# Returned rows of the first experts: an accumulating transfer of GpSimd in place of a load and VectorE's add

## The chip, the core and the metric

The kernel runs on one core of one Trainium2 chip. Its engines are TensorE (PE, with its weight loads PEld), VectorE (DVE), ScalarE (ACT), GpSimd (POOL) and SyncE (SP), which here only issues transfers. The metric is the time of the program on the device in microseconds (us), as the median of repeated runs.

## What is computed

The kernel is a decoder of two layers on `x` of 8 batches, 256 tokens and 256 features, all in float32. Each of six blocks normalizes the rows and adds its result to `x`:

```
x = x + L0_attn(layernorm(x))             # 16 heads
x = x + L0_xattn(ctx, layernorm(x))       # 16 heads, no weights
x = x + L0_ffn(layernorm(x))              # the first experts
x = x + L1_attn(layernorm(x))             # causal
x = x + L1_xattn(layernorm(x), ctx)
x = x + L1_ffn(layernorm(x))              # the second experts
```

The change is in the third block:

```
g = sinkhorn(x @ gate_w, 8 iterations)          # 256 tokens x 8 experts
vals, idx = top_k(g over tokens, 32)            # each expert chooses 32 tokens
out = (x[idx] @ experts[e]) * vals
back = zeros.at[idx].set(out)                   # a token chosen by several experts keeps the last one
```

so that `x + back` is the input of the second layer.

## The kernel before

The residual rows stay in SBUF for the whole run, in the tile `x` of 128 partitions by 16 row tiles by 256 features; batch b owns the row tiles 2b and 2b+1. The first two layers' attentions are 24 units: for each pair of batches two self attentions and two cross attentions of the first layer, then eight causal self attentions of the second layer. Their score products (`st`, L330), exponentials (`pT`, L341) and value products (`o`, L367) give the beat, four steps to a unit. Between the steps stand jobs, in an order written out by hand in `order_of_jobs`: `st16` takes the statistics of unit 16 (L249), `no16` normalizes (`xn`, L258, on POOL), `ro16` transposes (`tr`, L287), and so on. `x0` to `x3` advance the first experts of one pair of batches by one step each, up to the next `yield` of the generator `chosen_experts`. Every engine, and each queue of transfers, follows this order strictly.

For one pair of batches the generator normalizes the rows (`xnb`), writes them to DRAM (`xn<-xnb`, L657), and makes eight rounds of the gates: a product `cs` on PE, then `rc`, `gc`, `rsum` and `rr` on DVE (L676 to L682). DVE picks the 32 best of each expert (`top`, L698 to L703). SP writes these to DRAM and loads them in other layouts (`slots`, `idx_row`, `by_half`). For each batch, POOL gathers the chosen rows (`gather`, L735) in two indirect transfers, PE transposes them (`tr<-rows`) and multiplies by the experts (`y`, L751), DVE works out which rows must go aside because a later expert chose the same token (`junk`, L763), ACT or DVE scales (`ys`), and POOL scatters the result in two indirect transfers (L785) to `returned[b]` in DRAM. The second scatter waits for the first.

Then SP loads the first 256 rows of `returned[b]` (L795, 256 KB) into the tile `back`, which has two buffers, and DVE adds it to `x` (L798). The reader of the sum is the `st` job of the second layer's unit of the same batch (L249).

SP's queue carries more than that: the loads `memk` and `memv` of the cross attentions (L534, L536), and, one expert for every second unit, `packs` (L235 to L240), which copies the second experts' weights, 2.1 MB for each, from DRAM to DRAM in another layout. When the last expert step is done, `weights_x` closes the pools of the first experts and loads the weights of the second cross attention in their room: `wkv_x`, `wq_x` and `wout_x` on POOL's queue (L826 to L828), `nkrow`, `nvcol`, `lns` and `lnb` on SP's (L831 to L838). `own` (L863, L864) is a small DVE product with `nvcol`.

Of the kernel before, what the change touches and what calls it, by code (L numbers as in the profile page):

```python
# [29 lines left out]
F32 = mybir.dt.float32  # L30
# [4 lines left out]
ALU = mybir.AluOpType  # L35
# [4 lines left out]
P = 128  # L40
B, S, D = 8, 256, 256
# [116 lines left out]
def plain(  # L158
# [4 lines left out]
    nc = tc.nc  # L163
# [118 lines left out]
    def transposed(rows, work, mm, tag, dst=None, bufs=2):  # L282

        ps = mm.tile([P, 2, 2 * P], F32, tag="mm", name="tr")
        for t in range(2):
            for c in range(2):
                nc.tensor.transpose(ps[:, c, t * P : (t + 1) * P], rows[:, t, c * P : (c + 1) * P], ident)  # L287
        if dst is None:
            dst = work.tile([P, 2, 2 * P], F32, tag=tag, name=tag, bufs=bufs)
        nc.scalar.copy(dst, ps)  # L290
        return dst
# [310 lines left out]
    bwork = w_exp.enter_context(tc.tile_pool(name="b2", bufs=2, side="right"))  # L602
# [8 lines left out]
    returned = [dram.tile([2 * S, D], F32, name=f"back{b}") for b in range(B)]  # L611
# [32 lines left out]
    def chosen_experts(b0, nb):  # L644
# [86 lines left out]
        def gather(b):  # L731
            gathered[b] = bwork.tile([P, 2, D], F32, tag="rows", name="rows")
            for h in range(2):
                q = 2 * b + h
                nc.gpsimd.indirect_dma_start(  # L735
                    out=gathered[b][:, h, :],
                    out_offset=None,
                    in_=kept[b][:, :],
                    in_offset=bass.IndirectOffsetOnAxis(ap=from_i[:, q : q + 1], axis=0),
                )  # L740
# [3 lines left out]
        for b in range(nb):  # L744
            rT = transposed(gathered[b], bwork, mm, "rT")
            yield
            y = mm.tile([P, 2, D], F32, tag="mm", name="y")
            for e in range(E):
                rows = slice(TOP * (e % 4), TOP * (e % 4) + TOP)
                for c in range(2):  # L750
                    nc.tensor.matmul(  # L751
                        y[rows, e // 4, :],
                        rT[:, c, TOP * e : TOP * (e + 1)],
                        experts[:, e, c, :],
                        start=c == 0,
                        stop=c == 1,
                    )
                if e == 3:
                    yield
            for h in range(2):  # L760
                q = 2 * b + h
                junk = bwork.tile([P, S], F32, tag="junk", name="junk")
                nc.vector.scalar_tensor_tensor(  # L763
                    junk,
                    idx_row[:, b, :],
                    col[:, 0, q : q + 1],
                    later[:, h, :],
                    ALU.is_equal,
                    ALU.mult,
                    accum_out=over[:, q : q + 1],  # L770
                )
            of_b = slice(2 * b, 2 * b + 2)
            nc.vector.scalar_tensor_tensor(to[:, of_b], over[:, of_b], 0.0, to[:, of_b], ALU.is_equal, ALU.mult)
            nc.vector.tensor_tensor(to_i[:, of_b], to[:, of_b], aside, ALU.add)
            ys = bwork.tile([P, 2, D], F32, tag="ys", name="ys")
            for h in range(2):
                q = 2 * b + h
                if b0:
                    nc.scalar.activation(ys[:, h, :], y[:, h, :], AF.Copy, scale=col[:, 1, q : q + 1])
                else:  # L780
                    nc.vector.tensor_scalar(ys[:, h, :], y[:, h, :], col[:, 1, q : q + 1], None, ALU.mult)
            yield
            for h in range(2):
                q = 2 * b + h
                nc.gpsimd.indirect_dma_start(  # L785
                    out=returned[b0 + b][:, :],
                    out_offset=bass.IndirectOffsetOnAxis(ap=to_i[:, q : q + 1], axis=0),
                    in_=ys[:, h, :],
                    in_offset=None,
                )  # L790
                if not h and b + 1 < nb:
                    gather(b + 1)
                yield
            back = bwork.tile([P, 2, D], F32, tag="back", name="back")
            nc.sync.dma_start(back, returned[b0 + b][:S].rearrange("(t p) d -> p t d", p=P))  # L795
            yield
            xb = x[:, 2 * (b0 + b) : 2 * (b0 + b) + 2, :]
            nc.vector.tensor_tensor(xb, xb, back, ALU.add)  # L798
            yield


# [122 lines left out]
    for n, u in enumerate(units):  # L924
# [20 lines left out]
        "tb0": lambda: by_dims(sinT1, wides[2]),  # L945
    }
    ex = [chosen_experts(2 * i, 2) for i in range(B // 2)]
    jobs |= {f"x{i}": partial(next, ex[i], None) for i in range(B // 2)}
    order_of_jobs = """
# [2076 lines left out]
```

## Time and profile before

| | before |
|---|---|
| median of 16 runs | 1130.0 us (1124.93 to 1135.34) |
| the profiled execution | 1129.51 us |
| its span, first to last instruction | 1127.7 us |
| mean granted TensorE clock | 0.994 |
| scatters to `returned` (L785, 16) | 176.8 to 341.7 us, 1.0 us each on POOL |
| loads of `back` (L795, 8) | 184.0 to 344.2 us, 0.37 us each to issue |
| adds (L798, 8) | 188.1 to 352.1 us, 0.68 us each |

The profile is one execution. A page of it lists the busy time of each engine, the chain of work that ended last, followed back from the end, and the costliest groups of instructions. Other views are a timeline of each engine (start, length, engine, line, operation, output and inputs, and in brackets the idle time before it and what ended it), busy times in chosen windows, and a list of who waited for whom. PE's busy time is modelled, so a full PE is not a PE at its peak. Times are in us from the start of the span.

### The profile page before, as it was taken

What the parts mean: (1) busy time and instruction counts of PE and PEld (TensorE: products, weight loads), DVE (VectorE), ACT (ScalarE), POOL (GpSimd) and SP (SyncE); (2) the same over time, 40 slices, a digit from 0 to 9 for tenths busy, and PEclk for the clock granted to TensorE, in tenths of its full rate; (3) what the DMA queues carried; (4) which work ended last, traced back from release to release, by engine and by line L of the source; (5) the groups of instructions that cost most, each with busy time, mean ns of one, the idle gap of its engine ahead of it and who ended that gap; (6) DMA issues with size and microseconds to landing.
All of it is one profiled execution on the core that took longest, in us unless ns stands there. A gap on an engine that the chain in (4) does not pass through costs nothing.

```text
span 1127.7 us, 34931 instructions
## 1 busy us (share of the span) xinstructions
PE 1083.7 (96%) x15186; PEld 712.6 (63%) x15186; DVE 592.3 (53%) x1573; ACT 460.7 (41%) x747; POOL 439.5 (39%) x519
## 2 busy tenths in 40 slices
PE   6999999998998999999999999999999999999997
PEld 3444545544544545676777776777775768888874
DVE  5576778878887446435444443434357572222213
ACT  4776767674554524242424232323232321322220
POOL 3456364647687414242424233333325133000014
PEclk9999999999999999999999999999999999999999
DMA  8048344234145100101010102020232045999924
GB/s 238 32 158 283 108 135 126 63 121 135 35 140 203 73 3 20 40 21 49 21 50 20 49 21 49 20 49 20 49 122 52 1 170 195 360 415 402 393 65 139
DMA packets 62819, 130.87 MB, mean 116 GB/s; under 512 B 9904, under 2 KB 45984, under 8 KB 58304
## 3 DMA queue, kind: packets, MB, share of 16 engines
q1 hardware_dynamic: 54944, 108.61, 28.4%
q0 software_dynamic: 4992, 16.92, 4.3%
q10 hardware_dynamic: 2720, 3.02, 0.8%
q8 instruction: 121, 1.98, 0.7%
q14 instruction: 42, 0.34, 0.1%
HBM read 110.03 MB, written 35.80 MB: 129 GB/s over the span
## 4 chain that ended last, share of the span: by engine, by line
PE 80%; DVE 9%; ACT 4%; POOL 2%; DMA 2%; issue 2%; SPq 0%; DVEq 0%; ACTq 0%; POOLq 0%
PE h L272 8%; PE k L272 7%; PE st L330 7%; PE v L272 6%; PE o L367 4%; PE wo L272 4%; PE ox L1594 4%; PE stx L1554 4%; PE out L2014 4%; PE out L1831 4%; PE h L1196 3%; PE q L272 3%; PE qk L278 3%; ACT pT L341 3%; PE ao L278 2%
## 5 line engine op out<-in xcount | busy, mean ns | idle before, releaser
L341 ACT ACTIVATE pT<-st 128x1024 f32<-128x1024 f32 (+1 forms) x128 | 110.4, 915 | 59.8 <-PE st L330 58.3
L367 PE MATMUL o<-pT,padv 128*32 128x256 f32 (+1 forms) x1536 | 96.6, 368 | 1.4 <-DVE by_q L383 1.0
L1560 POOL TENSOR_TENSOR both<-pTx 128x512 f32<-128x512 f32 x64 | 87.4, 1395 | 21.1 <-ACT pTx L1558 19.1
L272 PE MATMUL h<-xrT,w 128*64 128x128 f32 (+1 forms) x1936 | 87.1, 250 | 0.7 <-issue 0.7
L272 PEld LDWEIGHTS h<-xrT,w 128*64 128x64 f32 x1936 | 84.5, 137 | 3.6 <-issue 1.3
L1189 DVE TENSOR_TENSOR midr<-sl,h 128x128 f32<-128x128 f32 x102 | 29.4, 288 | 101.8 <-PE h L272 69.2
L341 ACT ACTIVATE pT<-st,kbias 128x1024 f32<-128x1024 f32 x64 | 67.8, 1111 | 31.5 <-PE st L330 29.8
L367 PEld LDWEIGHTS o<-pT,padv 128*32 128x32 f32 x1536 | 44.4, 110 | 53.4 <-issue 22.6
L1558 ACT ACTIVATE pTx<-stx 128x1024 f32<-128x1024 f32 x64 | 62.5, 1023 | 31.4 <-PE stx L1554 28.1
L1188 ACT ACTIVATE sl<-h 128x128 f32<-128x128 f32 (+1 forms) x114 | 35.3, 310 | 95.0 <-PE h L272 56.0
L330 PE MATMUL st<-qm,kT 32*128 32x512 f32 (+1 forms) x512 | 67.3, 594 | 5.2 <-ACT qm L309 2.1
L278 PE MATMUL qk<-xnT,l_wqkv 128*32 128x256 f32 x1024 | 66.9, 387 | 0.8 <-issue 0.8
L1554 PE MATMUL stx<-qTx,kTx 64*128 64x256 f32 x512 | 64.4, 391 | 2.1 <-ACT pTx L1558 2.1
L1594 PE MATMUL ox<-pTx,vx 128*32 128x256 f32 x1024 | 63.2, 380 | 0.0
L1649 POOL TENSOR_TENSOR oT<-oT,rs 128x512 f32<-128x512 f32 x30 | 37.6, 1286 | 61.9 <-DMA rs<-rd 61.9
L383 DVE STREAM_TRANSPOSE by_q<-o 128x512 f32<-128x512 f32 x48 | 34.0, 709 | 51.2 <-PE o L367 51.0
L1554 PEld LDWEIGHTS stx<-qTx,kTx 64*128 64x128 f32 x512 | 46.1, 186 | 20.4 <-issue 7.0
L254 POOL TENSOR_TENSOR lxrs<-lxve,mhalf 128x2 f32<-128x2 f32 x8 | 5.6, 705 | 127.6 <-DVE lxve L252 127.6
L346 POOL TENSOR_SCALAR_AFFINE_SELECT pT<-pT 128x512 f32<-128x512 f32 x64 | 41.7, 671 | 29.9 <-ACT pT L341 29.5
L278 PEld LDWEIGHTS qk<-xnT,l_wqkv 128*32 128x32 f32 x1024 | 33.5, 112 | 28.6 <-issue 9.8
L2014 PE MATMUL out<-w,midr 128*64 128x256 f32 x408 | 47.6, 380 | 1.5 <-issue 1.3
L1602 DVE COPY oT<-ox 128x512 f32<-128x512 f32 x16 | 11.0, 689 | 72.3 <-PE ox L1594 72.3
(397 smaller groups left out, 2240.9 us busy)
## 6 DMA issues: line engine op xcount, KB each, us to landing
w<-packs SPq DMA_DIRECT2D x22, 1408.0 KB
w<-packs SPq DMA_DIRECT2D x22, 768.0 KB
rs<-rd SPq DMA_DIRECT2D x16, 512.0 KB
packs<-L_ffn_w_eDF SPq DMA_DIRECT2D x8, 704.0 KB
packs<-L_ffn_w_eDF SPq DMA_DIRECT2D x8, 640.0 KB
packs<-L_ffn_w_eFD SPq DMA_DIRECT2D x8, 640.0 KB
ctxT<-ctx_T SPq DMA_DIRECT2D x8, 512.0 KB
wkv_x<-L_xattn_Wkv POOLq DMA_DIRECT2D x1, 4096.0 KB
```

The source lines that it names most:

```text
L272: nc.tensor.matmul(out[h], lhsT[:, h], rhs, start=start, stop=stop, skip_group_check=True)
L278: nc.tensor.matmul(out[h : h + HP], lhsT[:, h : h + HP], rhs, start=start, stop=stop, skip_group_check=True)
L330: nc.tensor.matmul(st[:, r, :, :n], self.kT[rows, c, bass.ts(kt, P)], self.qm[rows, :, c, q0:], start=True, stop=True,)
L341: nc.scalar.activation(pT[:, :, :, :n], st[:, 2 * k : 2 * k + 2, :, :n], AF.Exp, scale=self.scale, **kb)
L346: nc.gpsimd.affine_select(out=pT[:, :, :, :P], in_=pT[:, :, :, :P], compare_op=ALU.is_ge, fill=0.0, base=0, pattern=[[0, 2], [0, 2], [1, P ...
L367: nc.tensor.matmul(o[HP * j : HP * j + HP, m, q0:], self.v_pad[:, kt, 8 * c + 2 * j + m, :], pTs[j // 2][:, j % 2, m, : S - q0], start=kt ...
L1554: nc.tensor.matmul(st[:, g, kt, :], kT[rows, c, bass.ts(kt, P)], qT[rows, c, :], start=True, stop=True)
L1558: nc.scalar.activation(pT, st, AF.Exp, scale=scale)
L1560: nc.gpsimd.tensor_tensor(both, pT[:, :, 0, :], pT[:, :, 1, :], ALU.add)
L1594: nc.tensor.matmul(o[at : at + HP, i, :], v[:, kt, 2 * (c2 + i) + g, lo : lo + HP], pT[:, g, kt, :], start=kt == 0, stop=kt == 1, skip_gro ...
L1831: nc.tensor.matmul(ps, mid[:, i, lo : lo + P], w2[:, i, :], start=i == 0, stop=i == NFC - 1)
L2014: nc.tensor.matmul(ps[h], mid[:, i, h], sets[k % len(sets)][1][:, i, :], start=i == 0, stop=i == NFC - 1, skip_group_check=True,)
```

## The change

The load of `back` on SP, the tile, and DVE's add are gone. At the place of the add, POOL issues one transfer from `returned[b]` to the rows of `x` that adds to its destination.

```diff
-            back = bwork.tile([P, 2, D], F32, tag="back", name="back")
-            nc.sync.dma_start(back, returned[b0 + b][:S].rearrange("(t p) d -> p t d", p=P))
             yield
             xb = x[:, 2 * (b0 + b) : 2 * (b0 + b) + 2, :]
-            nc.vector.tensor_tensor(xb, xb, back, ALU.add)
+            nc.gpsimd.dma_start(xb, returned[b0 + b][:S].rearrange("(t p) d -> p t d", p=P), accum_op=ALU.add)
             yield
```

The steps of the generator stay as many as they were, so the hand-written order is the same; the step that held the load is empty. In the order of instructions PE and ACT are as before; DVE has lost its eight adds, SP its eight loads, and POOL has eight more transfers. One instruction has moved: L864 now stands right behind L863 on DVE, where ten others stood between them. The transfer waits for the second scatter to land, and the first statistics of the batch wait for the transfer.

## The prediction

> **What bounds the kernel now.** I read the page first: the parts on busy time, the slices and the chain. TensorE holds the end, but the change lies between 176 and 358 us, so I then read that stretch by windows, by the chain in order of time, and by each engine's timeline.
>
> From the page:
>
> ```profile
> span 1127.7 us, 34931 instructions
> PE 1083.7 (96%) x15186; PEld 712.6 (63%) x15186; DVE 592.3 (53%) x1573; ACT 460.7 (41%) x747; POOL 439.5 (39%) x519
> PE 80%; DVE 9%; ACT 4%; POOL 2%; DMA 2%; issue 2%; SPq 0%; DVEq 0%; ACTq 0%; POOLq 0%
> ```
>
> Time is gained only where PE now stands idle in this stretch, and lost wherever PE is made to wait anew. The windows (columns: length, then PE, PEld, DVE, ACT, POOL busy, granted clock, DMA share, GB/s):
>
> ```profile
> 180.00:190.00 10.00, 10.00 (x228) 5.84 (x220) 7.18 (x23) 9.12 (x13) 3.91 (x5) 1.00 0.56 146
> 190.00:200.00 10.00, 9.64 (x187) 5.08 (x190) 9.04 (x33) 7.31 (x11) 6.58 (x8) 1.00 0.54 192
> 270.00:275.00 5.00, 2.33 (x24) 1.14 (x16) 4.93 (x11) 1.04 (x2) 4.81 (x6) 1.00 0.56 202
> 275.00:280.00 5.00, 5.00 (x60) 2.47 (x52) 0.86 (x5) 2.87 (x5) 3.04 (x4) 0.66 0.16 56
> ```
>
> At 190 us PE and DVE are both nearly full and feed each other. At 271 us there is the one real hole, and after it the granted clock falls to 0.66. The timelines of DVE, POOL and PE at the first add (batch 0):
>
> ```profile
> 188.09 0.67 DVE L798 TENSOR_TENSOR x<-x,back 128x512 f32<-128x512 f32 x1
> 188.80 0.43 DVE L249 BATCH_NORM_STATS2 lnst<-x 128x6 f32<-128x256 f32 x1
> 190.59 0.18 DVE L682 RECIPROCAL rr<-rsum 128x4 f32<-128x4 f32 x1
> 188.28 1.62 POOL L419 TENSOR_TENSOR qs<-qs,sinT 128x512 f32<-128x512 f32 x1 [4.94 <-DVE qs L416]
> 191.13 0.44 PE L278 MATMUL cs<-g,rr 128*32 128x8 f32 x32
> ```
>
> The statistics L249 read batch 0's rows at once after the add, and PE's `cs` product waits for `rr`, five DVE steps later. Last, from the chain, the two transfers that hold DVE and PE up today:
>
> ```profile
> 236.51 5.49 DMA back<-ys,to_i
> 242.02 2.85 DMA back<-back
> 267.29 6.73 DMA rows<-xn,from_i
> ```
>
> **What goes.** Eight adds on DVE (median 0.68 us, about 0.6 of it serial, since neighbours overlap), their 4.0 us of waits for the load, and eight loads on SP (0.37 us to issue). SP's gain is larger than that: its L795 waits for the scatter to land, 94.5 us in eight times, and the weight copies `packs`, `memk`, `memv` and `nkrow` stand behind it. They move forward.
>
> **What comes.** Eight issues on POOL at the places of the old adds. No row shows an accumulating transfer. Issue: the nearest row is the direct `xr` load, 0.55 us; upward, an indirect one at 1.0. Issue to landing: at the low end 2.4 to 2.6 (scatters of 128 KB in quiet), or 2.85 for the same 256 KB through SP; at the high end 6.5 to 7.1, which `rows` gathers take under a `packs` copy. A cost below nothing is excluded, since each add's reader now waits for a transfer where it waited for a 0.67 us instruction. I take 4.0: the 2.85 row plus about 1 us, because the transfer must also read its destination.
>
> The Trainium skill, DMA: Bandwidth & Descriptors, "Anatomy of one DMA — SWDGE (gpsimd) path", fits a plain GpSimd transfer as 2.0 us plus bytes over 436 GB/s; an estimate from it is 2.6 us for 256 KB, which would take 1.4 us off each wait below, and it prices no accumulation. Its "Rules for kernel authors" say to issue a transfer early and wait on it late, which speaks against this change.
>
> **Term 1, batch 0: +6.1.** POOL reaches the accumulating transfer when L419 ends, at 189.7 to 189.9; it lands at 193.7. DVE stands at L249 until then, with the whole router iteration queued behind it. From the start of L249 to the end of `rr` take 2.0 us (188.80 to 190.77), so `rr` comes at 195.7. PE is ready for `cs` at 191.1 and runs in order, so it is idle for 4.6 us. The clock follows: after the hole of 2.03 and 0.64 us at 271, 32 matmuls of `y` took 3.55 us, against 1.97 at full clock. I add 1.5. At a landing of 2.6 the hole is 3.2, at 7.0 it is 7.6.
>
> The Trainium skill, TensorE: Matmul & The Clock Gate, "What's actually happening", puts the threshold at an idle window of about 3.4 us; the row at 271 shows the fall after shorter holes, so I go by the row. By the page a hole of 3.2 might cost no clock, the forecast's 4.6 would.
>
> **Term 2, batch 2's gathers: +1.0 (0 to 3.5).** Without batch 1's load, which waits until 229.4, the next `packs` copy follows `memv` at 212.5 instead of 229.9. It takes 10 to 11 us (230 to 240 in the windows), so the gathers at 218.9 and 220.3 now run in its tail. Gathers at the same distance from a copy's start, 315.4 and 317.0 after 309.2, took 4.6 and 3.1; PE wants the rows at 223.2. So 0.3 to 2 us, or 3.5 if they take 6.6 as those at 232.5 did.
>
> **Term 3, batches 1, 2 and the hole at 271: -2.9 (0 to -5.6).** The scatters at 229.9 and 236.5 are then quiet. The second accumulating transfer goes at 233.7 and lands near 237.7, when its reader (238.35 less one add) comes. The third goes behind `lnrs`, at about 240.1, and lands at 244.1; the reader stood at 246.56, so DVE gains 2.5. PE has only 1.5 to 1.8 of idle to give back before 265. The gathers at 265.9 come 1.5 earlier, and the `packs` copy of 262.2 some 6 earlier, since batch 3's load no longer holds it; they land at 268.8 and the hole closes. That would be worth 5.6 at the end of `y`. But POOL is full there (4.81 of 5): second `xnb`, then 0.8 for the fourth issue, then the selects that the next `o` product needs. That brings `o` to 276.0 instead of 278.9.
>
> **Term 4, batch 4: +0.5 (-0.6 to +1.2).** Issue at 296.5, after `xn`; landing 300.5; the reader is due at 299.3 to 299.9. POOL's selects behind it slip by 0.1 to 0.3.
>
> **Term 5, batches 5 to 7: +2.3 (0 to +4).** Batch 5's transfer comes behind the scatter and its gap, at 331.5, and lands at 335.5; its reader was at 331.2. DVE is 4.3 late, POOL's `xn` ends at 340.4 instead of 336.1, and PE's transposes of it, due at 336.6, wait 3.8 and lose 1.5 of clock. Part comes back: DVE's `own` product now stands right behind its reduction (338.0), and its operand `nvcol` is loaded sooner, so the 2.57 us wait at 346.4 and PE's holes of 1.33 (350.5) and 1.62 (356.1) go. I followed DVE to `kT` L473 before 356: PE is 2.3 late there. Batch 6's landing is hidden by that delay, batch 7's (351.1 plus 4) by DVE's work until 358.1.
>
> Batch 3 costs nothing but the 0.8 in term 3: its reader comes at 291.6, 15 us after the issue. If that cover were gone it would cost a landing, 4.0.
>
> **Sum.** 6.1 + 1.0 - 2.9 + 0.5 + 2.3 = 7.0. The profiled execution took 1129.5 us (span 1127.7), so 1136.5; it lies 0.5 under the median of the runs, so 1137.0. After 360 us PE has no holes to absorb a shift, so it stays to the end.
>
> **Rivals.** *The transfer is as slow in quiet as gathers are under load (7 us).* For it: a read, an add and a write for each element, which no row shows. Against: quiet rows are all near 3. Price: 9.1, 1.0, then batches 1 and 2 turn from gain to +3.4, 4.2 and 5.3: +23, 1153. *SP's freedom outweighs the waits, so it is faster.* The landing is 2.6, batch 0's hole is 3.2 and costs no clock, the gathers lose nothing, the hole at 271 closes wholly (-5.6), batch 4 gains 0.6, batches 5 to 7 come out even: -3.0, 1127.0. It decides where batch 0's hole stays below about 3.4, that is a landing below 2.8. For it are the 94.5 us of SP's waits; against it stands POOL's full stretch at 270. *It cancels:* batch 0 as in the last case with the clock lost (+4.7), term 3 at -4.5: within 0.2%.
>
> **The numbers.** A measurement of this kernel can tell about 0.2%, 2.3 us. Forecast (+2.3 to +12): 0.54. Slow transfer (beyond +12): 0.20. Cancelled: 0.13. Faster: 0.13. So slower 0.74, same 0.13, faster 0.13. At a landing of about 5.7 us the same sums give some +15; the range goes from 1129 to 1146 and leaves out the faster case and the upper third of the slow one.
>
> **What would show it.** Right: DVE's longest wait at L249, on a transfer `x<-back`, about 4 us near 189; a PE hole of 4 to 5 us before `cs` and a clock below 1.00 after it; `packs` issued near 180 and 219; no 2 us hole before `tr<-rows` near 271; a second wait at L249 near 332. Wrong: issue to landing of `x<-back` outside 3 to 5 us; the hole at 271 still there although `packs` moved; PE waiting in the gathers near 223; a shift that is given back after 360.

## The result, and the profile after

The changed kernel took 1141.84 us (median of 11 runs, 1138.14 to 1142.25) beside 1129.36 for the kernel before (62 runs). The ratio is 1.010, with a 95% interval of 1.0084 to 1.0115, so the change costs 9.5 to 13.0 us. The forecast was 1137.0, that is +7.0, with a range of 1129 to 1146: the result lies inside the range, and the forecast itself below the interval. The profiled execution has a span of 1138.9, 11.2 above the one before.

From the page after:

```profile
span 1138.9 us, 34920 instructions
PE 1087.9 (96%) x15186; PEld 715.5 (63%) x15186; DVE 592.4 (52%) x1565; ACT 460.9 (40%) x747; POOL 450.9 (40%) x527
PE 81%; DVE 7%; ACT 4%; DMA 3%; POOL 3%; issue 2%; SPq 0%; DVEq 0%; ACTq 0%; POOLq 0%
```

DVE has eight instructions fewer and is no less busy (592.4 against 592.3): the eight adds of 0.68 us are gone, and other DVE instructions have become longer by as much. POOL has eight more, for 11.4 us: 1.4 for each. In the chain, DMA has gone from 2% to 3%. The windows (columns as before: length, PE, PEld, DVE, ACT, POOL busy, granted clock, DMA share, GB/s):

```profile
190.00:200.00 10.00, 5.07 (x76) 3.02 (x76) 3.41 (x14) 3.76 (x5) 5.32 (x6) 0.73 0.35 85
270.00:275.00 5.00, 4.92 (x82) 2.70 (x78) 4.83 (x12) 2.05 (x4) 4.47 (x5) 1.00 1.02 380
285.00:290.00 5.00, 3.49 (x102) 1.75 (x100) 3.76 (x8) 2.29 (x5) 4.57 (x6) 1.00 0.36 56
```

At 190 us PE has fallen from 9.64 to 5.07 of ten, at a clock of 0.73: this is the largest loss. At 285 us there is a second one, which the prediction did not have. The timelines at batch 0 (start, length, engine, line; in brackets the idle time before it and what ended it):

```profile
190.55 1.36 POOL L796 DMA_DIRECT2D x<-back  x1
195.04 0.43 DVE L249 BATCH_NORM_STATS2 lnst<-x 128x6 f32<-128x256 f32 x1 [5.79 <-DMA x<-back]
197.16 0.81 PE L278 MATMUL cs<-g,rr 128*32 128x8 f32 x30 [4.91 <-DVE rr L682]
199.45 1.98 PE L278 MATMUL v<-l_wqkv,xnT 128*32 128x256 f32 x16
```

POOL issues at 190.55, DVE's reader starts 4.5 us later, and PE is idle for 4.91 us because `rr` is queued behind the reader. Then `v` takes 1.98 us instead of 1.07, at a granted clock of 0.50. The same pattern came back at batch 5, and PE's work at the old hole of 271 now runs through:

```profile
279.06 0.67 PE L287 MATMUL tr<-ident,rows 128*128 128x128 f32 x4 [0.75 <-DMA rows<-xn,from_i]
280.73 1.97 PE L751 MATMUL y<-experts,rT 128*32 128x256 f32 x32
342.88 0.43 DVE L249 BATCH_NORM_STATS2 lnst<-x 128x6 f32<-128x256 f32 x1 [4.88 <-DMA x<-back]
344.80 1.94 PE L367 MATMUL o<-pT,padv 128*32 128x256 f32 x16 [4.17 <-DVE by_q L383]
```

Matching PE's instructions of the two profiles one by one gives the lateness of the profile after at each point, here by the time in the profile before. It is +1.0 at 190 (before the first transfer, so this belongs to the execution), +7.9 at 212, +8.2 at 242, +7.6 at 264, +3.6 at 279, +5.8 at 282, +6.8 at 309 and +10.2 from 366 on. After that nothing is given back, and the end is within 1 us of that.

The waits of DVE and SP (line, who ended the wait: total, times, longest):

```profile
DVE lnst L249 <- DMA x<-back: 13.3, 4, 5.8
SPq L706 <- DVE top L703: 106.5, 4, 39.7
```

All of the new wait on DVE stands in four readers: batches 0, 2, 4 and 5, with 5.79, 2.04, 0.54 and 4.88. SP's 94.5 us of waiting for scatters are gone, but its wait for `top` rose from 54.8 to 106.5.

### The profile page after: what moved, and what is told of

The parts are those of the page before. It is cut to its first block, busy times and chain, and to the rows that moved or that the text cites. A ratio compares the mean times of both kernels' runs of the same rounds, so it can differ in the third digit from the quotient of the medians.

```text
span 1138.9 us, 34920 instructions
## 1 busy us (share of the span) xinstructions
PE 1087.9 (96%) x15186; PEld 715.5 (63%) x15186; DVE 592.4 (52%) x1565; ACT 460.9 (40%) x747; POOL 450.9 (40%) x527
## 3 DMA queue, kind: packets, MB, share of 16 engines
q8 instruction: 121, 1.98, 0.7%
## 4 chain that ended last, share of the span: by engine, by line
PE 81%; DVE 7%; ACT 4%; DMA 3%; POOL 3%; issue 2%; SPq 0%; DVEq 0%; ACTq 0%; POOLq 0%
PE h L272 7%; PE st L330 7%; PE k L272 7%; PE v L272 6%; PE o L367 5%; PE stx L1552 4%; PE ox L1592 4%; PE wo L272 4%; PE out L2012 4%; PE out L1829 4%; PE h L1194 3%; PE qk L278 3%; PE q L272 3%; ACT pT L341 3%; PE ao L278 2%
## 5 line engine op out<-in xcount | busy, mean ns | idle before, releaser
L367 PE MATMUL o<-pT,padv 128*32 128x256 f32 (+1 forms) x1536 | 98.9, 373 | 7.0 <-DVE by_q L383 5.6
L383 DVE STREAM_TRANSPOSE by_q<-o 128x512 f32<-128x512 f32 x48 | 34.0, 709 | 46.9 <-PE o L367 46.7
L346 POOL TENSOR_SCALAR_AFFINE_SELECT pT<-pT 128x512 f32<-128x512 f32 x64 | 45.2, 794 | 24.1 <-ACT pT L341 24.1
L249 DVE BATCH_NORM_STATS2 lnst<-x 128x6 f32<-128x256 f32 x96 | 38.7, 406 | 21.9 <-DMA x<-back 13.3
```

The source lines that it names most:

```text
L346: nc.gpsimd.affine_select(out=pT[:, :, :, :P], in_=pT[:, :, :, :P], compare_op=ALU.is_ge, fill=0.0, base=0, pattern=[[0, 2], [0, 2], [1, P ...
L367: nc.tensor.matmul(o[HP * j : HP * j + HP, m, q0:], self.v_pad[:, kt, 8 * c + 2 * j + m, :], pTs[j // 2][:, j % 2, m, : S - q0], start=kt ...
```

## The experiments

Times are medians; the change against before comes from the ratio, in us, with its interval. The first four kernels ran on a chip on which the kernel before took 1129.67, the others on one where it took 1141 to 1142, so times are compared within a group, by the ratio to before. The changed kernel itself was timed on the first chip alone, so where a kernel of the second group is set beside it, the two changes against before are compared. In the second group the kernel before was timed but not profiled.

### Batch 0 alone, batches 1 to 3, batches 4 to 7

```diff
+            by_add = b0 + b == 0        # or: in (1, 2, 3); or: >= 4
+            if not by_add: (tile back, load on SP)
             yield
+            if by_add:
+                nc.gpsimd.dma_start(xb, returned..., accum_op=ALU.add)
+            else:
                 nc.vector.tensor_tensor(xb, xb, back, ALU.add)
```

> Batch 0 alone goes by the accumulating transfer; batches 1 to 7 keep the load on SP and VectorE's add. Theory (the loss is where a reader stands right behind the transfer): DVE waits at L249 some 5.8 us near 190, PE has one hole of 4 to 5 us before cs, and the time is +6 to +7.5, about 1136. The gathers of batch 2 and the hole at 271 stay as before, because batch 1's load still holds SP. Rival 1 (the loss is spread evenly, each of the eight transfers costing 12.5 / 8 = 1.6 through its issue on POOL): +1.6, 1131. Rival 2 (the shift is absorbed later by PE's holes at 236 to 271): under +3.

> Batches 1, 2 and 3 alone go by the accumulating transfer. Theory (SP is freed early, the hole before the transposes of the gathered rows at 271 closes and the clock there stays up): -1 to -3, about 1127.5, with the packs copy of 262 issued some 2 us earlier against PE and a hole under 1 us at 271. Rival 1 (the gain in the profile of the changed kernel came only because batch 0's stall had moved everything, and without it the gathers meet the copy as before): within 1 of no change, hole of about 2 us still there. Rival 2 (each transfer costs 1.6): +4.8, 1134.

> Batches 4 to 7 alone go by the accumulating transfer. Theory by the terms on record: +0.5 and +2.3, so +2.8, 1132; by the two profiles, +1.0 and +3 to +3.5, so +4 to +4.5, 1133.5, with a DVE wait of 4 to 5 us at L249 for batch 5 and a PE hole of about 4 us before an o product. Rival (each transfer costs 1.6): +6.3, 1135.7. If the parts e1, e2 and e3 add up to the whole change (+12.5), nothing else moves the time.

| | time | ratio (interval) | change |
|---|---|---|---|
| batch 0 | 1136.41 | 1.0054 (1.0032 to 1.0075) | +6.1 (3.6 to 8.5) |
| batches 1 to 3 | 1130.23 | 1.0004 (0.9984 to 1.0024) | +0.5 (-1.8 to 2.7) |
| batches 4 to 7 | 1133.48 | 1.0034 (1.0013 to 1.0055) | +3.8 (1.5 to 6.2) |

The three add up to +10.4, within the interval of the whole change. So one transfer of eight carries about half of the loss, and an even price of 1.6 per transfer is refuted: batch 0 would have cost 1.6, batches 1 to 3 4.8. The PE timelines, first with batch 0 alone, then with batches 1 to 3:

```profile
195.96 0.79 PE L278 MATMUL cs<-g,rr 128*32 128x8 f32 x30 [4.75 <-DVE rr L682]
279.05 1.35 PE L287 MATMUL tr<-ident,rows 128*128 128x128 f32 x4 [2.25 <-DMA rows<-xn,from_i]
```

```profile
273.62 0.67 PE L287 MATMUL tr<-ident,rows 128*128 128x128 f32 x4 [0.76 <-DMA rows<-xn,from_i]
221.73 0.39 PE L278 MATMUL cs<-g,rr 128*32 128x8 f32 x26 [1.87 <-issue]
```

With batch 0 alone the hole of the gathers stays (2.25); with batches 1 to 3 it shrinks to 0.76, and PE is 1.9 early by the profiles at 279. Yet the kernel of batches 1 to 3 gains nothing: a new gap of 1.87 at 221 and a stretched product at 279 (below) give it back. Another 1.5 us of its profile went near 190, where batch 0's plain add waited 0.84 us for its load; up to there the program is that of the kernel before, so this belongs to the execution. The expected gain of 1 to 3 was not seen.

### SP held as before

```diff
+            back = bwork.tile([P, 2, D], F32, tag="back", name="back")
+            nc.sync.dma_start(back, returned...)
             yield
             nc.gpsimd.dma_start(xb, returned..., accum_op=ALU.add)
```

> The changed kernel with SP's loads kept: they still wait for the scatters and fill a tile that nobody reads, while the accumulating transfer does the adding. So SP's queue is held as before, and the change keeps only its costs. Theory (the freedom of SP is worth 3 us at the hole of 271, and something in batches 5 to 7): 3 to 5 slower than the changed kernel, 1145 to 1147, with a hole of 2 us back before the transposes of the gathered rows. Rival (the hole closed because the third transfer's reader and the gathers came relatively earlier, not because of SP): within 1 of the changed kernel, 1142.

Measured: 1149.7, ratio 1.0177 (1.0144 to 1.0210), +20.0. That is 8 above the changed kernel, where 3 to 5 were expected, so SP's freedom is worth more than the theory had. The hole before the transposes of the gathered rows came back at 1.72 us. The profile is of the fastest of the six runs, 5.6 under their median, so it shows only part of the loss. POOL and DVE at batch 0 in this kernel, and SP's copy just ahead of them:

```profile
185.35 0.60 SPq L235 DMA_DIRECT2D packs<-L_ffn_w_eDF  x1
187.21 1.35 POOL L798 DMA_DIRECT2D x<-back  x1
196.27 0.43 DVE L249 BATCH_NORM_STATS2 lnst<-x 128x6 f32<-128x256 f32 x1 [10.36 <-DMA x<-back]
```

The `packs` copy starts 1.9 us ahead of the transfer, and the reader starts 9.1 us after the issue. In the changed kernel the copy began at 181.65 and the transfer came 8.9 us later, when the copy was nearly through: 4.5 us. Batch 1's transfer met the next copy in the same way, 3.3 us behind its start, and its reader started 8.9 us after the issue. So SP's freedom also kept batch 0's landing short, by 4.6 us. The added loads move 2.1 MB more, which this kernel does not separate from the hold.

### The same transfer without the adding

```diff
-            nc.gpsimd.dma_start(xb, returned..., accum_op=ALU.add)
+            nc.gpsimd.dma_start(xb, returned...)
```

> The changed kernel without the adding: GpSimd's transfer overwrites the rows of x with the returned rows at the same place, so the residual is left out of these rows. Everything else, the places in the queues and the waits, is as in the changed kernel. Theory (reading the destination and adding is what makes the transfer 1.5 us longer than the 2.85 us load on SP): DVE's waits on x<-back fall by about 1.5 each, the wait of batch 0 to some 4.3, and the time is 2 to 4 below the changed kernel, 1138 to 1140. Rival 1 (any direct transfer of this shape from GpSimd's queue takes 4.5, adding or not): within 1 of 1142, issue still 1.35. The slow product att (L387, 3.15 us at 284) tells of another thing: if it stays, it comes from the issue on POOL and what follows it there, not from the adding.

Its total, 1271.28 (ratio 1.1135, 1.1112 to 1.1159), says nothing on the change, since with other residual rows the second experts' routing, and so their work, is another. Up to 360 us the program is the same. POOL and DVE there:

```profile
189.63 0.80 POOL L796 DMA_DIRECT2D x<-back  x1
192.62 0.43 DVE L249 BATCH_NORM_STATS2 lnst<-x 128x6 f32<-128x256 f32 x1 [4.29 <-DMA x<-back]
194.73 0.59 PE L278 MATMUL cs<-g,rr 128*32 128x8 f32 x29 [3.41 <-DVE rr L682]
283.45 3.43 DVE L387 TENSOR_TENSOR att<-by_q,dens 128x256 f32<-128x256 f32 x1
```

The issue takes 0.79 to 0.85 us instead of 1.27 to 1.41, and the reader starts 3.0 us after it (2.99, 3.08, 3.09 and 3.07 in the four that were waited for) instead of 4.5 to 4.8. DVE's waits on `x<-back` fall from 13.3 to 6.9 us. So adding costs 1.5 us in the landing and 0.5 in the issue. The packets differ too: the queue of POOL's transfers carries 2176 packets more than before for the eight accumulating transfers, 272 each, and 640 more, 80 each, for the eight plain loads of the kernel below, for the same 2.1 MB. The stretched `att` stays, as the rival condition foresaw: it doesn't come from the adding.

### Issued one step earlier, and a plain load on GpSimd

```diff
-            yield
             xb = x[:, 2 * (b0 + b) : 2 * (b0 + b) + 2, :]
             nc.gpsimd.dma_start(xb, returned..., accum_op=ALU.add)
+            yield
             yield
```

> The changed kernel with each accumulating transfer issued one step earlier, at the place of the old load, straight behind the second scatter. POOL then stands until the scatter has landed, some 2.5 us, before it issues. Theory (the loss is the landing in front of a reader): batch 0's transfer is issued at about 186 instead of 190.5, lands at 190.5, DVE's wait there falls from 5.8 to about 1 and term 1 from 6.9 to 1 or 2; batch 5's wait falls little, its places being close together. Time 1134 to 1137. Rival (what is saved at the readers is lost on POOL, whose selects, rotary products and gathers queue behind eight waits of 2.5): 1140 to 1145.

Measured: 1145.28 beside 1141.89, ratio 1.0031 (1.0014 to 1.0048), +3.5. That is at or below the theory's +4 to +7, and the rival's +10 to +15 is out. POOL at batch 0:

```profile
184.35 1.35 POOL L795 DMA_DIRECT2D x<-back  x1 [1.12 <-DMA back<-ys,to_i]
193.62 0.43 DVE L249 BATCH_NORM_STATS2 lnst<-x 128x6 f32<-128x256 f32 x1 [2.80 <-DMA x<-back]
```

The issue is 6 us earlier, but DVE's wait fell only from 5.79 to 2.80, since the transfer now runs beside the copy issued at 183.38 and takes 9.3 us. In the 4.5 to 4.8 us of the changed kernel it would have landed before DVE was ready at 190.8; no run shows that. PE's hole of 1.92 there cost no clock (`v` behind it 1.07).

```diff
-            nc.sync.dma_start(back, returned...)
+            nc.gpsimd.dma_start(back, returned...)
             yield
             nc.vector.tensor_tensor(xb, xb, back, ALU.add)
```

> The kernel before with the load of back issued by GpSimd instead of SP, at the same place; VectorE's add stays. So SP is as free as in the changed kernel, no reader stands behind an accumulation, and POOL stands through each scatter's landing (2.5 us, eight times) and issues for 1.3. Theory: it keeps the gain at the hole of 271 and pays nothing near 190, 1127 to 1130. Rival (POOL's standing and issuing costs as much as SP's freedom is worth, above all near 270 and 330): 1131 to 1136. If it is as slow as the changed kernel, 1142, POOL's queue and not the reader's place is what costs.

Measured: 1153.51, ratio 1.0108 (1.0084 to 1.0132), +12.3: the same as the changed kernel's change. The expectation had named this case, and had read it as POOL's queue being what costs and not the reader's place. The runs do not bear that reading out: batch 0 alone costs 6.1, and without the three close readers (next section) the loss goes, with five issues still on POOL. What this kernel shows is that freeing SP does not pay by itself when POOL takes the loads over. DVE's adds of batches 5 and 7 wait 5.38 and 4.40 us, because on POOL batch 5's load (343.46) stands behind two gathers and a scatter: again a reader close behind a landing. Those explain part of it; PE was already later than in the other kernels of this group at 240 us, with the granted clock at 0.50 from 241.91 to 248.74, and why is not settled.

### Without the three readers that wait, and only the three that are clear of everything

The edit is that of the first three kernels, with `not in (0, 2, 5)` and `in (1, 6, 7)`.

> Batches 1, 3, 4, 6 and 7 go by the accumulating transfer; batches 0, 2 and 5, whose readers waited 5.8, 2.0 and 4.9 us for it, keep the load on SP and VectorE's add. Theory (readers close behind are the whole loss): no wait over 1 us on x<-back, 1128 to 1131, no worse than before. Rival (the issues on POOL, 1.35 us each, and the slow product behind batch 3's cost by themselves): +2 to +5, 1132 to 1135.

> Batches 1, 6 and 7 alone go by the accumulating transfer, the three whose readers never waited for it and whose issues did not stand beside a stretched product. Theory: SP is freed of batch 1's wait, nothing waits, so 0 to 2 under before. Rival (what SP's freedom moves, the copy into the gathers of batch 2 and of batches 4 to 6, costs as much as it gains): within 1 of before, or above.

Measured: 1142.87 beside 1141.89, ratio 1.0008 (0.9991 to 1.0024), +0.9 (-1.0 to 2.7); and 1143.23 beside 1141.34, ratio 1.0016 (1.0000 to 1.0031), +1.8 (0.0 to 3.5). Five of the eight transfers are free within what can be measured, as the theory said, though batch 4's reader waited 1.39 us and the rival's +2 lies inside the interval. Neither kernel is faster than before, so the gain of 0 to 2 that the last theory had is not there; its rival, within 1 of before or above, has the number. Both have a gap in PE's issue at 221 (0.70 and 1.31 us) and a DVE wait for `nvcol` (6.30 and 5.18 us); that these take up what SP's freedom gains was not separated. No version that was run beats the kernel before.

### The readers moved instead

```diff
-        cv11 | x0 va12 hb13 rb13 x0 st16
+        cv11 | x0 va12 hb13 rb13 x0
...
-        x1 | vb12 no16 x1
+        x1 st16 | vb12 no16 x1
...
-        x2 st17 no15 | x1 x1 x2 cv15 st18
-        be15 | x1 x1
+        x2 st17 no15 | x1 x1 x2 cv15
+        be15 | x1 x1 st18
...
-        ob17 ob18 x3 st21 | va20 vb20 no21 x3 x3
+        ob17 ob18 x3 | va20 vb20 st21 no21 x3 x3
```

> The changed kernel with three readers moved later in the hand-written order: the statistics of batch 0 (st16) by about 8 us, of batch 2 (st18) by about 4, and of batch 5 (st21) by a few DVE instructions, each still ahead of the step that uses them. The transfers stay where they are. Theory (the loss is a landing of 4.5 us with a reader straight behind it): the waits at L249 for batches 0 and 2 go, the PE hole of 4.9 before cs goes with its clock, batch 5's wait shrinks from 4.9 to 2 or 3; of the changed kernel's +12 against before at most +4 is left. Rival (the transfers' issues on POOL and what they do to DVE beside them carry most of it): +7 or more is left.

> The kernel before (load on SP, VectorE's add) with the same three readers moved later: the control for the two runs beside it. Theory: the readers had no wait on a transfer there, apart from the add's own 4.0 us in two places, so no change beyond 1.5 either way. Rival (the moved readers help or harm by themselves, by what else they stand beside): over 2 either way, and then the other two are to be read against this one.

The second kernel with batch 3's transfer at the step before:

```diff
+            if b0 + b == 3:
+                nc.gpsimd.dma_start(xb, returned..., accum_op=ALU.add)
             yield
-            nc.gpsimd.dma_start(xb, returned..., accum_op=ALU.add)
+            if b0 + b != 3:
+                nc.gpsimd.dma_start(xb, returned..., accum_op=ALU.add)
             yield
```

> As the kernel with three readers moved, and batch 3's transfer issued one step earlier, where DVE's product att (L387) does not stand beside it. Theory (the 3.15 us that this product took in every run with batch 3's transfer in its later place, against 0.42 elsewhere, costs PE about 2 us before cs): 1.5 to 2.5 under the kernel with three readers moved, no VectorE product over 1.2 us between 270 and 295. Rival (PE would have stood there anyway, for POOL's selects): within 0.5 of it.

| readers moved | time | ratio (interval) | change |
|---|---|---|---|
| load and add, as before | 1145.68 | 1.0040 (1.0022 to 1.0059) | +4.6 |
| accumulating transfer | 1149.12 | 1.0070 (1.0055 to 1.0086) | +8.0 |
| the same, batch 3 a step earlier | 1146.63 | 1.0048 (1.0035 to 1.0061) | +5.5 |

Before was 1141.34. Against before, the second row is the rival's number; but the control shows that the moved readers cost 4.6 by themselves, which its theory had excluded. Against the control the accumulating transfer costs some 3.4, where on the other chip it cost 11 with the readers in place, and 0.9 when batch 3's goes a step earlier as well. This points to two places, the readers close behind a landing and batch 3's issue. It is a difference of differences, and that the moved readers cost the same 4.6 with either way of adding was not shown. Nor did the waits go, as the theory had it. DVE and PE near batch 0 with the readers moved:

```profile
196.58 0.43 DVE L249 BATCH_NORM_STATS2 lnst<-x 128x6 f32<-128x256 f32 x1 [2.75 <-DMA x<-back]
198.40 1.07 PE L367 MATMUL o<-pT,padv 128*32 128x256 f32 x16 [2.48 <-DVE by_q L383]
```

The transfer was issued at 190.76, so this reader started 5.8 us after it. DVE's waits on `x<-back` fell from 13.3 to 8.2 us only, and the hole on PE from 4.91 to 2.48, now before another product. That the moved readers cost something makes this no better kernel.

### The stretched product

DVE and POOL at batch 3's transfer in the changed kernel, and PE's wait that follows:

```profile
283.12 1.35 POOL L796 DMA_DIRECT2D x<-back  x1
284.21 3.15 DVE L387 TENSOR_TENSOR att<-by_q,dens 128x256 f32<-128x256 f32 x1
285.22 1.76 POOL L466 TENSOR_TENSOR qr<-qc,qs 128x512 f32<-128x512 f32 x1
287.95 0.44 PE L278 MATMUL cs<-g,ones 128*32 128x8 f32 x32 [1.09 <-DVE g L665]
```

In the changed kernel `att` takes 0.42 to 0.72 us in 46 of its 48 places; one takes 1.51, as in the kernel before, and this one 3.15. Here it took 3.15, 3.15, 3.43, 3.52 and 3.35 in every kernel that issues batch 3's transfer at this place with SP free, and 0.89 in the one with SP held. With batch 3's transfer a step earlier it is back at its own length, and that kernel is 2.5 us faster by the medians (the two intervals just overlap). With all eight a step earlier it took 0.84. The lines are of these two kernels:

```profile
284.57 0.43 DVE L387 TENSOR_TENSOR att<-by_q,dens 128x256 f32<-128x256 f32 x1
285.02 0.84 DVE L387 TENSOR_TENSOR att<-by_q,dens 128x256 f32<-128x256 f32 x1
```

In the changed kernel the product ends at 287.36, 0.38 us after POOL's `qr` (286.98). With batches 1 to 3 alone it ends at 281.93, 0.39 after `qr` (281.54), and 0.38 after it in the kernel without batches 0, 2 and 5. That looks as if it ran its 0.42 us at once when `qr` was over. In the kernel before, POOL was idle from 279.58 to 281.55 and `att` ran in that pause at 280.63. In all five long cases `att` began while POOL's issue of the transfer was still running, 0.03 to 0.62 us before its end, and the selects and `qr` followed at once. With SP held it began 1.9 us after the issue had ended, and the 0.84 above began 0.08 us after the first select (284.94), with no issue beside it. So meeting the selects alone does not make it long; whether the issue holds it or the three operations behind the issue was not separated.

The Trainium skill, SBUF — State Buffer, "SBUF: two separate sides", says that a DVE instruction with two SBUF inputs and a GpSimd instruction that reads SBUF take one shared pair of ports by an exclusive lock: who comes first keeps it for the whole instruction. The ends of `att` agree with that in four of the five cases (0.38 or 0.39 us after `qr`; 0.88 in the fifth); the lock itself no run here shows.

## Why the prediction was right, term by term

**The price of one transfer.** Assumed: issue 0.55 to 1.0, landing 4.0, the 2.85 row plus 1 us for reading the destination. Measured: issue 1.35, landing 4.5 to 4.8. The mechanism was right, both sizes were low; the plain transfer's 3.0 shows that the 1 us for the destination is 1.5. The estimate of 2.6 from the Trainium skill's fit (DMA: Bandwidth & Descriptors, "Anatomy of one DMA — SWDGE (gpsimd) path") is 0.4 under what the plain transfer took here.

**Term 1, +6.1.** Measured +6.1 by batch 0 alone and +6.9 between the two profiles: DVE's longest wait at L249 near 190, a hole of 4.91 (said 4.6), and 2.1 lost at the lower clock (said 1.5), of which 0.2 came back.

**The clock rule.** I went by the row at 271 (holes of 2.03 and 0.64, then `y` at 3.55) against the window of about 3.4 us that the Trainium skill gives in TensorE: Matmul & The Clock Gate, "What's actually happening". The length of a hole decides it in neither way. The granted clock fell to 0.50 after holes of 1.74 (changed kernel, at 167), 2.03 with 0.64 (before) and 2.25 (batch 0 alone, the transposes at 279 above: 1.35 us instead of 0.67). It held after 1.76 (batches 1 to 3, at 166), 1.96 (batches 4 to 7, at 273) and 2.93:

```profile
166.96 0.41 PE L278 MATMUL cs<-g,rr 128*32 128x8 f32 x29 [1.74 <-DVE rr L682]
348.68 1.07 PE L278 MATMUL v<-l_wqkv,xnT 128*32 128x256 f32 x16 [2.93 <-DVE x L502]
```

The second line is of the kernel with the load on GpSimd. In the traces the clock's changes stand multiples of 3.41 us apart. Cut on that grid, the 14 profiles have 1134 stretches between 100 and 420 us. After all 17 in which PE was busy (as modelled) for under 0.42 of the time, the next stretch had half the clock; after those from 0.42 to 0.53 it was 15 of 19, after the busier ones 7 of 1098. So the window has the page's length, but a stretch of it that is half busy can already bring the clock down, and a hole of some 2 us costs 1.7 or nothing by where it falls. Term 1 was safe: by these figures, as an estimate, a hole of over 4 us leaves one stretch under 0.42 wherever it falls. The row at 271 went by where its hole fell, and that is part of term 3.

**Term 2, +1.0.** The size was right (+0.9 by the profiles), but by luck: the mechanism was not. PE did not wait for the gathers near 223. It stood in the middle of a group of `cs`:

```profile
227.60 0.39 PE L278 MATMUL cs<-g,rr 128*32 128x8 f32 x25 [0.67 <-issue]
```

The DMA view of the changed kernel between 224 and 229 us (queue: packets, MB, share of 16 engines) has SP's queue, with the `packs` copy, on all DMA engines:

```profile
q1 hardware_dynamic: 1353, 1.80, 101.1%
```

A gap of 0.39 to 1.87 us with no releaser stands before this `cs` in all nine kernels in which batch 1 doesn't hold SP, the one with the load on GpSimd among them, and in none of the other five. In all nine it ends 1.2 to 1.5 us after the last packet (16 KB) of the queue that the DMA view calls `instruction`; in the other five that packet had ended 1.75 to 2.97 us before the same `cs`. So the copy seems to delay the loading of instructions; no run changed that alone, and it is not shown.

**Term 3, -2.9.** The profiles give -3.0: the hole at 271 shrank to 0.75 with no clock lost, +3.6 at 279, and 2.2 was lost again at 282. The sum came out by luck, for two steps were wrong. The copy of 262 was to come some 6 us earlier; it came 2.4 earlier relative to PE, since behind the load SP's queue had another wait, that of `slots` for `top` (L706). And the give-back came not where POOL's selects release `o` at 276, but through DVE's `att` at 284. Tried alone, batches 1 to 3 gave +0.5: about 1.6 of the -3.0 is `y` at full clock (1.97 against 3.55), and with batches 4 to 7 alone `y` also took 1.97 with the old holes in place (1.96 and 0.47). The stretch of the clock's grid that holds the hole was busy for 0.55 there and for 0.52 in before. So that part belongs to where the hole fell in the profiled execution of before, not surely to the change.

**Terms 4 and 5, +0.5 and +2.3.** Measured together +3.8, and by the profiles +1.1 and +3.6. The step that failed is what I put behind DVE's wait at batch 5. I counted the path over POOL's `xn` to PE's transposes at 336.6. Nearer by was `by_q` (L383), queued on DVE behind L249, and with it PE's `o`: a hole of 4.17 and 1.7 of clock, 2.8 us sooner in the order of before (`o` at 333.86, the transposes at 336.64). Part was given back as said, between 349 and 366. `own` did not stop waiting: it stood 2.07 for `y` and 3.81 for `nvcol`.

**The sum.** +7.0 was forecast and +11.2 measured between the profiles, 9.5 to 13.0 by the runs. So the direction and the largest term were right and the sum was 2.5 to 6 us low; the wide range took that up. By the profiles term 1 is 0.8 low, term 5 1.3, term 4 0.6; 1.0 is lateness that the profile after had before the first transfer; the rest is the difference between single executions. The rival of a slow transfer (7 us in quiet) is refuted by 4.5 to 4.8; it did take 8.9 to 9.3 beside a copy. The rival that SP's freedom outweighs the waits has its right half, since holding SP again costs 8, and fails at its condition, a landing below 2.8.

## What to carry to other kernels

A transfer that replaces a load and an add is priced by its whole latency at the place of its reader: find for each instance what reads the sum next on the same engine, and what stands in the queue behind that reader. Five of eight readers had room here and cost nothing measurable, and one without room cost half of all. When a queue is freed, look for the next wait in it before counting the gain.

## What the runs showed of the hardware that was not expected

- An accumulating transfer of 256 KB from DRAM to SBUF went in 272 packets against 80 for a plain one, with 1.35 us to issue against 0.8 and 4.5 to 4.8 us to its reader against 3.0 to 3.1. In other kernels it took 4.0 to 5.8, and 7.9 twice beside the loads of `ctxT`.
- The same transfer took 9.3, 9.1 and 8.9 us to its reader when it was issued 1.0, 1.9 and 3.3 us after the start of a 2.1 MB copy.
- A VectorE product of 0.42 us took 3.15 to 3.52 in the five kernels where it began during the issue of a GpSimd transfer with three GpSimd operations behind it.
- PE's clock changed only on a grid of 3.41 us. It fell after stretches in which PE was busy for under 0.42 (17 of 17) and mostly after 0.42 to 0.53 (15 of 19), so holes of 1.74 to 2.25 us cost clock in some executions, and one of 2.93 did not.
- Gaps of 0.39 to 1.87 us on PE, beside a 2.1 MB copy, ended 1.2 to 1.5 us after a 16 KB packet of the instruction queue in nine of nine kernels.
